# Block 1 to 3 adapter products in float32r from split parts, and the order of Silu and of up's PSUM bank, in a fused LoRA + FP8 gated FFN

## Chip, cores and metric

The kernel runs on one core of one Trainium2 chip. The metric is device time in microseconds of one launch; the figure for the kernel before is the median of 3 runs, 475.9 us (475.79 to 476.99).

## What is computed

For each of 8 sequences of 256 tokens and 1024 features, a LoRA adapter of rank 16 (chosen by an id) replaces the input of a gated feed-forward layer, and the layer's output is added to x:

```
Bx  = x @ B[id].T                     # 1024 -> 16
c   = Bx @ A[id].T                    # 16 -> 1024
xq  = fp8(c / in_scale) * in_scale
hid = silu(xq @ gate.T) * (xq @ up.T) # 1024 -> 2752
out = x + fp8(hid / s) * s @ down.T   # 2752 -> 1024
```

Weights hold values of float8 (e4m3) as float32, and the products Bx and c are float32 in the reference.

## The kernel before, in words

Tokens are laid along the free axis in 4 blocks of 512 (two sequences each, t = 0 to 3), features along the 128 partitions. The 2752 hidden features are NI = 22 chunks of 128, the last with 64.

Each block goes through: B's product (bx), a copy of it to SBUF (bm), A's product (c, in PSUM), and a rounding of c to fp8 with the input scale (xg, 8 feature slabs of 512 tokens). Then for every chunk c and block t, `gate_up` (L580 to L628) does 8 matmuls into a gate bank and 8 into an up bank (y, 128x512), Silu on ACT (g, L610), and the product with up on DVE (hid, L611). The down projection (yd) follows with the same TensorE shapes, and DVE adds x (o, L696).

All TensorE instructions are issued through `multiply` (L469 to L471), which fixes their program order; so all matmuls and weight loads have line L471 in the profile and are told apart by tile names. Other engines' instructions are placed by the framework's scheduler unless they are held with `keep_in_program_order`. Tiles of PSUM come from one pool of 8 banks with one tag: a new tile takes the bank that has been free or is freed first, and its first matmul waits for the reader of the old tile.

B's products use four 32-column strips of the array, A's four 32-row strips, one per sequence (or half of one), so four products stand side by side. In float32, each program instruction of these shows as two matmul and two weight load records.

- Block 0: `two_times_b(0)`, `two_times_a(0, bm)` at the start, with empty products (warm) between.
- Block 1: `two_times_b(1)` is put after 12 of the 16 matmuls of `gate_up(4, 0)`. Each DVE and ACT copy of L517 moves 64 partitions by 128 columns, once straight and once to the other half of the partitions, so that A's products (L531 to L551, 32x128) find all columns. `two_times_a` does 2 parts of four banks each; a part is 16 products of 128 columns. Its banks are rounded by ACT (L529) and DVE (L527) in turn.
- Blocks 2 and 3: `four_times_b` stands after 8 of the 16 matmuls of `gate_up(3, 1)` and `four_times_a` does four banks per pair of feature slabs, 8 products of 16 rows and 256 columns each: pairs 0 and 1 after `gate_up(3, 1)`, pairs 2 and 3 after 8 of 16 matmuls of `gate_up(4, 1)`.

After that come blocks 2 and 3 of chunks 0 to 4, all four blocks of chunks 5 to 21, then down. `NFIRST` is 5.

Loads are issued on SP in the order of the code and wait for one of eight queue slots: x and B and A of block 0, gate and up weights of chunks 0 to 4, B of block 1 (L366), x of block 1 in two pieces of 7 and 1 slabs (L381), A of block 1 (L373), x and B of blocks 2 and 3, A of blocks 2 and 3 (L420). GpSimd only sets constants.

Of the kernel before, what the change touches and what calls it, by code (L numbers as in the profile page):

```python
# [8 lines left out]

F32 = mybir.dt.float32  # L10
BF16 = mybir.dt.bfloat16
FP8 = mybir.dt.float8e4
U16 = mybir.dt.uint16
I32 = mybir.dt.int32
AF = mybir.ActivationFunctionType
ALU = mybir.AluOpType
AX = mybir.AxisListType

P = 128
# [264 lines left out]
def adaln_ffn(  # L284
# [4 lines left out]
    aT: bass.AP,  # L289
    bT: bass.AP,  # L290
    a8: bass.AP,
    b8: bass.AP,
    w_gu: bass.AP,
    w_d: bass.AP,
# [27 lines left out]
    kept = ctx.enter_context(tc.tile_pool(name="kept", bufs=1))  # L322
    wpool = ctx.enter_context(tc.tile_pool(name="w", bufs=5))
    outs = ctx.enter_context(tc.tile_pool(name="outs", bufs=3))
    hid = [kept.tile([P, T], FP8, name=f"hid{c}") for c in range(NI - 1)]


    hid_tail = kept.tile([P, 2, TB], BF16, name="hid_tail")
# [8 lines left out]
    with ExitStack() as fast:  # L337
# [17 lines left out]
        b_four = lora.tile([P, 4 * BROW + R], F32, name="b_four")  # L355
        a_four = lora.tile([P, H], F32, name="a_four")
        nc.gpsimd.memset(a_two[0], 0.0)
        nc.vector.memset(a_two[1], 0.0)
        for b, n in ((b_two[0], 2), (b_two[1], 2), (b_four, 4)):
            nc.vector.memset(b[:, n * BROW :], 0.0)  # L360

# [8 lines left out]
        def load_a_two(t, j, adapter, queue=nc.sync):  # L370
            for g in range(2):
                row = 32 * (2 * g + j) + R * j
                queue.dma_start(  # L373
                    out=a_two[t][row : row + R],
                    in_=a8[bass.ds(adapter * 2 * R + g * R, R), :],
                )

        def load_x(t, k):
            piece, first = x_of(x4, t, k)
            ks = slice(first, first + piece.shape[1])  # L380
            nc.sync.dma_start(out=xs[t][:, ks, :], in_=piece)  # L381
# [25 lines left out]
        adapters = [adapter_of(2 + q, nc.sync) for q in range(6)]  # L407
        for j in range(2):
            load_b(b_two[1], j, adapters[j], nc.sync)
        for k in (0, 7):  # L410
            load_x(1, k)
        for j in range(2):
            load_a_two(1, j, adapters.pop(0))

        for t in (2, 3):
            load_x(t, 0)
            for q in (2 * t - 4, 2 * t - 3):
                load_b(b_four, q, adapters[q], nc.sync)
        for q in range(4):
            nc.sync.dma_start(  # L420
                out=a_four[32 * q : 32 * q + R], in_=aT[bass.ds(adapters[q] * R, R), :]
            )


        sc = b_two[0][:, NH * R : BROW]
# [58 lines left out]
        def times_b(bx, b, n, quads, between=None):  # L484


            for k in range(NH):
                for q, (i, row, t, cols) in enumerate(quads):
                    at = i * BROW + k * R - row
                    multiply(  # L490
                        bx[q][32 * q : 32 * (q + 1)],
                        lhsT=b[:, at : at + 32],
                        rhs=xs[t][:, k, cols],
                        start=(k == 0),
                        stop=(k == NH - 1),
                    )
                if between:
                    between(k)

        def two_times_b(t, between=None):  # L500


            n = SEQ // 2
            quads = [
                (j, R * j, t, slice(at, at + n))
                for half in range(2)
                for j in range(2)
                for at in (j * SEQ + half * n,)
            ]
            bx = [psum.tile([P, n], F32, tag="ps", name=f"bx{half}") for half in range(2)]  # L510
            times_b([bx[q // 2] for q in range(4)], b_two[t], n, quads, between)
            bm = lora.tile([P, 2, n], F32, tag="bm2", name="bm2", bufs=2)
            for other in range(2):
                for half, copy in enumerate((nc.vector.tensor_copy, nc.scalar.copy)):
                    to = half ^ other
                    tc.keep_in_program_order(
                        copy(  # L517
                            bm[64 * to : 64 * (to + 1), other],
                            bx[half][64 * half : 64 * (half + 1)],
                        )  # L520
                    )
            return bm

        def round_to(to, c, engine):
            scale = inv[:, GATE_IN : GATE_IN + 1]
            if engine is nc.vector:
                nc.vector.tensor_scalar(to, c, scale, None, ALU.mult, saturate=False)  # L527
            else:
                nc.scalar.activation(to, c, AF.Copy, scale=scale, saturate=False)  # L529

        def two_times_a(t, bm):  # L531


            n = SEQ // 2
            for part in range(2):
                cs = [psum.tile([P, 2, SEQ], F32, tag="ps", name=f"c{q}") for q in range(4)]
                for other, i in product(range(2), range(2)):
                    for q in range(4):
                        rows = slice(32 * q, 32 * (q + 1))
                        multiply(  # L540
                            cs[q][:, i, bass.ts(q // 2 ^ other, n)],
                            lhsT=a_two[t][rows, bass.ts(2 * part + i, P)],
                            rhs=bm[rows, other],
                            start=True,
                            stop=True,
                        )
                for q in range(4):
                    k = KS * part + 2 * (q // 2)
                    to = xg[t][:, k : k + 2, bass.ts(q % 2, SEQ)]
                    round_to(to, cs[q], nc.vector if q % 2 else nc.scalar)  # L550

        def four_times_b():
            quads = [(q, 0, 2 + q // 2, bass.ts(q % 2, SEQ)) for q in range(4)]
            bx = psum.tile([P, SEQ], F32, tag="ps", name="bx")
            times_b([bx] * 4, b_four, SEQ, quads)
            bm = lora.tile([P, SEQ], F32, tag="bm", name="bm", bufs=2)
            nc.vector.tensor_copy(bm, bx)
            return bm

        def four_times_a(bm, pairs):  # L560
            for i in pairs:
                cs = [psum.tile([P, 2, SEQ], F32, tag="ps", name=f"c{q}") for q in range(4)]
                for k in range(2):
                    for q in range(4):
                        rows = slice(32 * q, 32 * q + R)
                        multiply(
                            cs[q][:, k],
                            lhsT=a_four[rows, bass.ts(2 * i + k, P)],
                            rhs=bm[rows],
                            start=True,  # L570
                            stop=True,
                        )
                for q in range(4):
                    to = xg[2 + q // 2][:, 2 * i : 2 * i + 2, bass.ts(q % 2, SEQ)]
                    round_to(to, cs[q], nc.vector if q % 2 else nc.scalar)
# [5 lines left out]
        def gate_up(c, t, turns=(NH,), between=None):  # L581
# [3 lines left out]
            w = w_of[c]  # L585
            cols = bass.ts(t, TB)
            js = range(1 if tail else 2)
            ys = [psum.tile([P, TB], F32, tag="ps", name=f"y{j}") for j in js]
            steps = []
            for i, n in enumerate(turns):  # L590
                done = sum(turns[:i])
                steps += product(js, range(done, done + n))
            for i, (j, k) in enumerate(steps):
                if between and i == between[0]:
                    between[1]()
                multiply(
                    ys[j],
                    lhsT=high(w[:, k if tail else k // KS * NH + j * KS + k % KS, :]),
                    rhs=xg[t][:, k, :],
                    start=(k == 0),  # L600
                    stop=(k == NH - 1),
                )
            gates, ups = (ys[0], ys[-1]) if not tail else (ys[0][:TAIL], ys[0][TAIL:])
            rows = slice(TAIL, P) if tail else slice(0, P)
            if tail:
                to = lora.tile([P, 2 * TB], FP8, tag="bm", name="tail", bufs=2)[half_of(t), :TB]
            else:
                to = hid[c][:, cols]
            g = work.tile([P, TB], F32, tag="g", name="g")
            nc.scalar.activation(g[rows], gates, AF.Silu, scale=gate_s[: gates.shape[0]])  # L610
            nc.vector.scalar_tensor_tensor(  # L611
                to,
                in0=ups,
                scalar=up_by_down[rows],
                in1=g[rows],
                op0=ALU.mult,
                op1=ALU.mult,
                saturate=False,
            )
            if tail:  # L620
                nc.vector.tensor_copy(hid_tail[half_of(t), t // 2], to)
# [11 lines left out]

        warm = psum.tile([P, TB], F32, tag="ps", name="warm")
        pass_time(warm, 16, TB)
        bm = two_times_b(0, lambda k: pass_time(warm, 4) if k == 6 else None)
        pass_time(warm, 7)
        two_times_a(0, bm)
        gate_up(0, 0, turns=(2, 2, 2, 2))
        for c in range(1, NFIRST - 1):  # L640
            gate_up(c, 0)
        bms = []
        gate_up(NFIRST - 1, 0, between=(12, lambda: bms.append(two_times_b(1))))
        two_times_a(1, bms[0])
        gate_up(0, 1, turns=(2, 2, 2, 2))
        for c in range(1, NFIRST - 2):
            gate_up(c, 1)
# [238 lines left out]
```

## Time and profile before

| | us |
|---|---|
| median of 3 runs | 475.9 |
| profiled execution, first to last instruction | 474.0 |
| bx and c of block 0 end, y begins | 12.1 |
| bx of block 1 begins | 28.9 |
| bx of blocks 2 and 3 begins | 46.0 |
| y of gate and up, 1376 matmuls, mean record | 0.379 |
| ACT rounding of a c bank, 128x512 | 0.69 |
| DVE rounding of a c bank | 0.75 |
| ACT / DVE copy of bx, 64x128 | 0.26 / 0.28 |
| POOL busy in all | 1.0 |

The page gives the span of the profiled execution, 474.0 us at a granted TensorE clock of 1.000, and no other time of that execution; the runs' median is 1.9 us above the span. Records of one engine overlap: a matmul record lasts longer than the distance to the next, so durations of matmuls are not to be added; distances between starts are. A line of the timeline has start, length from first start to last end, engine, line, operation, tiles, count and, in brackets, the idle time before it and what ended it.

### The profile page before, as it was taken

To read this page: it belongs to the slowest core of one execution; us is meant where nothing else is said; L and a number is where in the kernel's file an instruction comes from. 1 tells how busy PE (TensorE), PEld (TensorE's weight loads), DVE (VectorE), ACT (ScalarE), POOL (GpSimd) and SP (SyncE) were. 2 spreads that over 40 slices of the span, in tenths; PEclk is the share of its full clock that TensorE was granted. 3 is DMA by queue.
4 is the path that set the end of the run, shared out by engine and by line. 5 is a ranking of instruction groups with operands and counts; after the bars stand their busy time and mean duration, and the time that the engine had idled before them with its cause. 6 is when DMAs were issued, how large, how long until landed. Compare 5 with 4: busy or idle time off the path is not lost.

```text
span 474.0 us, 6007 instructions
## 1 busy us (share of the span) xinstructions
PE 469.6 (99%) x2514; PEld 217.1 (46%) x2514; DVE 105.6 (22%) x163; ACT 192.5 (41%) x249; POOL 1.0 (0%) x7
## 2 busy tenths in 40 slices
PE   8999999999999999999999999999999999999997
PEld 5454544444444444444444444444444444444444
DVE  2332521212212121222212121232120121031031
ACT  2332438995555745443354544359212022021000
POOL 0000000000000000000000000000000000000000
DMA  8995023322222112222210121133335255163031
GB/s 316 416 406 153 1 90 115 153 89 90 89 89 90 54 45 80 90 89 89 90 57 36 41 62 56 61 100 106 115 135 162 66 184 160 28 212 110 3 116 67
DMA packets 13781, 53.45 MB, mean 113 GB/s; under 512 B 1650, under 2 KB 2930, under 8 KB 10802
## 3 DMA queue, kind: packets, MB, share of 16 engines
q1 hardware_dynamic: 13536, 52.86, 31.8%
q8 instruction: 21, 0.34, 0.3%
q10 hardware_dynamic: 210, 0.14, 0.1%
q14 instruction: 14, 0.11, 0.1%
HBM read 44.60 MB, written 8.39 MB: 112 GB/s over the span
## 4 chain that ended last, share of the span: by engine, by line
PE 96%; DMA 2%; ACTq 0%; ACT 0%; issue 0%; DVE 0%
PE y L471 62%; PE yd L471 32%; DMA w_gu<-w_gu 1%; PE c L471 1%; PE bx L471 1%; DMA a<-a 1%; ACT L307 0%; ACTq L373 0%; ACTq L306 0%; ACTq L366 0%; DVE o L696 0%; ACTq L363 0%; PE count L471 0%
## 5 line engine op out<-in xcount | busy, mean ns | idle before, releaser
L471 PE MATMUL y<-xg,w_gu 128*128 128x512 fp8e4 x1376 | 298.2, 379 | 0.1
L471 PEld LDWEIGHTS <-w_gu 128*128 128x128 bf16 x1376 | 134.1, 98 | 162.8 <-issue 1.3
L471 PE MATMUL yd<-hid,w_d 128*128 128x512 fp8e4 (+2 forms) x693 | 146.0, 373 | 0.0
L610 ACT ACTIVATE g<-y,gate_s 128x512 f32<-128x512 f32 (+1 forms) x88 | 59.8, 681 | 136.3 <-PE y L471 136.3
L611 DVE SCALAR_TENSOR_TENSOR hid<-y,up_by_down,g 128x512 fp8e4<-128x512 f32 x84 | 63.1, 751 | 219.4 <-PE y L471 161.6
L471 PEld LDWEIGHTS <-w_d 128*128 128x128 bf16 x693 | 66.6, 98 | 79.0 <-issue 1.7
L457 ACT ACTIVATE junk<-w_d 128x1408 bf16<-128x1408 uint16 (+1 forms) x16 | 21.2, 1324 | 88.5 <-DMA w_d<-w_d 88.4
L696 DVE SCALAR_TENSOR_TENSOR o<-yd,down_s,x 128x512 f32<-128x512 f32 x28 | 20.0, 748 | 107.3 <-PE yd L471 92.5
L457 ACT ACTIVATE junk<-w_gu 128x2048 bf16<-128x2048 uint16 (+1 forms) x22 | 41.0, 1863 | 0.0
L464 ACT ACTIVATE junk<-hid 128x2048 bf16<-128x2048 fp8e4 x21 | 40.0, 1904 | 0.4
L464 ACT ACTIVATE junk<-xg 128x2048 bf16<-128x2048 fp8e4 x8 | 15.3, 1909 | 0.3
L529 ACT ACTIVATE xg<-c,inv 128x512 fp8e4<-128x512 f32 x16 | 9.7, 688 | 8.6 <-PE c L471 8.6
L527 DVE TENSOR_SCALAR xg<-c,inv 128x512 fp8e4<-128x512 f32 x16 | 10.9, 745 | 2.8 <-PE c L471 2.8
L471 PE MATMUL warm<-zeros 128*128 128x512 bf16 (+1 forms) x27 | 6.6, 404 | 1.2 <-DVE zeros L309 1.2
L696 DVE SCALAR_TENSOR_TENSOR o<-yd,down_s,xg 128x512 f32<-128x512 f32 (+2 forms) x5 | 3.2, 644 | 12.3 <-PE yd L471 12.3
L517 ACT COPY bm<-bx 64x128 f32<-64x128 f32 x4 | 1.0, 262 | 9.2 <-PE bx L471 9.2
L471 PEld LDWEIGHTS <-zeros 128*128 128x128 bf16 x27 | 2.6, 117 | 4.8 <-issue 3.1
L471 PE MATMUL bx<-x,b 128*32 128x128 f32 x128 | 4.3, 276 | 0.1
L471 PE MATMUL c<-bm,a 32*128 32x128 f32 x128 | 4.3, 277 | 0.0
L457 ACT ACTIVATION_READ_ACCUMULATOR junk<-w_gu 128x1 f32 x22 | 4.2, 191 | 0.0
L471 PEld LDWEIGHTS c<-bm,a 32*128 32x128 f32 x128 | 3.9, 186 | 0.5 <-ACT bm L517 0.4
L471 PE MATMUL yd<-hid_tail,w_dt 64*128 64x512 bf16 (+1 forms) x32 | 4.1, 377 | 0.0
(47 smaller groups left out, 41.0 us busy)
## 6 DMA issues: line engine op xcount, KB each, us to landing
w_gu<-w_gu SPq DMA_DIRECT2D x20, 1024.0 KB, 4.8
outT<-o SPq DMA_DIRECT2D x31, 256.0 KB, 2.2
w_d<-w_d SPq DMA_DIRECT2D x8, 704.0 KB, 4.9
w_d<-w_d SPq DMA_DIRECT2D x8, 640.0 KB, 3.9
x<-x SPq DMA_DIRECT2D x2, 2048.0 KB, 11.3
x<-x SPq DMA_DIRECT2D x1, 1792.0 KB, 13.1
w_gu<-w_gu SPq DMA_DIRECT2D x3, 512.0 KB, 4.2
x<-x SPq DMA_DIRECT2D x2, 512.0 KB, 3.9
```

Source lines behind the costliest of these rows:

```text
L457: nc.scalar.activation(junk_like(w), low(w), AF.Copy, accum_out=lows[:rows, column : column + 1])
L464: nc.scalar.activation(junk_like(q), q, AF.Square, accum_out=squares[:rows, column : column + 1])
L471: tc.keep_in_program_order(nc.tensor.matmul(*args, **kwargs))
L517: copy(bm[64 * to : 64 * (to + 1), other], bx[half][64 * half : 64 * (half + 1)],)
L527: nc.vector.tensor_scalar(to, c, scale, None, ALU.mult, saturate=False)
L529: nc.scalar.activation(to, c, AF.Copy, scale=scale, saturate=False)
L610: nc.scalar.activation(g[rows], gates, AF.Silu, scale=gate_s[: gates.shape[0]])
L611: nc.vector.scalar_tensor_tensor(to, in0=ups, scalar=up_by_down[rows], in1=g[rows], op0=ALU.mult, op1=ALU.mult, saturate=False,)
L696: nc.vector.scalar_tensor_tensor(o, in0=y, scalar=down_s, in1=x, op0=ALU.mult, op1=ALU.add)
```

## The change

1. A of block 1 to 3 is loaded with each sequence's 16 rows twice in 32 partitions (arrays `a8_twice`, `a_twice`). GpSimd splits it into float32r parts: lanes 0 to 15 of each 32 get A rounded to float32r, lanes 16 to 31 get the rest. For that it makes a scalar per partition (`lane`, `minus`) with an iota and two DVE instructions.
2. B of block 1 to 3 is copied by GpSimd so that each slab's 16 columns stand twice side by side; B's products then give Bx in both halves of 32 partitions.
3. Bx is split into two float32r parts, bm and rest, by a copy and a subtraction. In block 1 four ACT copies from SBUF then move each part's columns to the other half of the partitions.
4. A's products take float32r operands of 32 rows and 256 columns: per bank two parts times two k (or feature slabs), 16 products for four banks. Blocks 2 and 3 had 8 of 256 columns in float32, block 1 had 16 of 128 columns.
5. Silu is issued in the code right behind the last gate matmul, and the tile of up's bank is taken when its first matmul is issued. For chunks below 5 Silu and hid's product keep their program order.
6. The new tiles lie in the places of hid tiles that are written later. Block 0 is as before.

The diff, cut to its core:

```diff
@@ loads
-        for k in (0, 7):
-            load_x(1, k)
+        load_x(1, 0)
         for j in range(2):
-            load_a_two(1, j, adapters.pop(0))
+            adapter = adapters.pop(0)
+            for g in range(2):
+                load_a_twice(a_two[1], 2 * g + j, a8_twice, adapter * 2 + g)
+        load_x(1, 7)
...
         for q in range(4):
-            nc.sync.dma_start(
-                out=a_four[32 * q : 32 * q + R], in_=aT[bass.ds(adapters[q] * R, R), :]
-            )
+            load_a_twice(a_four, q, a_twice, adapters[q])
@@ GpSimd
+        lane = const.tile([P, 1], I32, name="lane")
+        nc.gpsimd.iota(lane, pattern=[[0, 1]], base=0, channel_multiplier=1)
+        nc.vector.tensor_scalar(lane, lane, R, None, ALU.bitwise_and)
+        minus = const.tile([P, 1], F32, name="minus")
+        nc.vector.tensor_scalar(minus, lane, -1.0 / R, None, ALU.mult)
+        def split(a, parts, cuts=1):
+            n = a.shape[1] // cuts
+            for cols in (bass.ts(i, n) for i in range(cuts)):
+                part = parts[:, cols]
+                nc.gpsimd.tensor_scalar(part, a[:, cols], minus, None, ALU.mult)
+                nc.gpsimd.tensor_tensor(part, a[:, cols], part.bitcast(F32), ALU.add)
+        def twice(b, n, name, slot):
...
+                for copy in range(2):
+                    nc.gpsimd.tensor_copy(to[:, :, copy], row)
...
+        b_twice = [twice(b_two[1], 2, "b_twice", NI - 2)]
+        split(a_two[1], a_parts[0], cuts=2)
+        b_twice.append(twice(b_four, 4, "b_four_twice", NI - 4))
+        for i in range(2):
+            split(a_four[:, bass.ts(i, H // 2)], a_parts[1 + i])
@@ block 1
+        def two_times_b_in_parts():
...
+            for half, copy in enumerate((nc.vector.tensor_copy, nc.scalar.copy)):
+                held(copy(bm[own[half], half], bx[half][own[half]]))
+            for half in range(2):
+                held(
+                    nc.vector.tensor_tensor(
+                        rest[own[half], half],
+                        bx[half][own[half]],
+                        bm[own[half], half].bitcast(F32),
+                        ALU.subtract,
+                    )
+                )
+            for part, half in ((bm, 1), (bm, 0), (rest, 0), (rest, 1)):
+                held(nc.scalar.copy(part[own[1 - half], half], part[own[half], half].bitcast(F32)))
@@ A's products, blocks 1 to 3
+        def times_a_parts(bms, a, at):
+            cs = [psum.tile([P, 2, SEQ], F32, tag="ps", name=f"c{q}") for q in range(4)]
+            for bm, i in product(bms, range(2)):
+                for q in range(4):
+                    rows = slice(32 * q, 32 * (q + 1))
+                    multiply(
+                        cs[q][:, i],
+                        lhsT=a[rows, bass.ts(at + i, P)],
+                        rhs=bm[rows],
+                        start=bm is bms[0] and i == 0,
+                        stop=bm is bms[-1] and i == 1,
+                    )
+            return cs
@@ blocks 2 and 3, behind B's product
             nc.vector.tensor_copy(bm, bx)
-            return bm
...
+            nc.vector.tensor_tensor(rest, bx, bm.bitcast(F32), ALU.subtract)
+            return bm, rest
@@ gate_up
-            ys = [psum.tile([P, TB], F32, tag="ps", name=f"y{j}") for j in js]
+            ys = []
...
+                if j == len(ys):
+                    ys.append(psum.tile([P, TB], F32, tag="ps", name=f"y{j}"))
                 multiply(
...
+                if j == 0 and k == NH - 1:
+                    silu()
```

## The prediction

> **What bounds the kernel now.** I read the busy shares first, then the chain of work that ended last in order of time, then the timeline around the three stretches the change edits.
>
> ```profile
> PE 469.6 (99%) x2514; PEld 217.1 (46%) x2514; DVE 105.6 (22%) x163; ACT 192.5 (41%) x249; POOL 1.0 (0%) x7
> ```
>
> TensorE is busy 469.6 of 474.0 us, so only time taken out of its own queue can shorten the run. The chain (start, us, what) shows how little of that queue the change can touch:
>
> ```profile
> 31.81 2.07 PE c L471 x64
> 33.87 12.19 PE y L471 x56
> 46.07 3.59 PE bx L471 x64
> 49.66 1.83 PE y L471 x8
> 51.49 2.04 PE c L471 x32
> 53.53 1.83 PE y L471 x8
> 55.37 1.94 PE c L471 x32
> 57.30 264.29 PE y L471 x1224
> ```
>
> The A products of block 1 (31.81) and of blocks 2 and 3 (51.49, 55.37) hold 2.07 + 2.04 + 1.94 = 6.05 us, 1.3% of the span. Everything from 57.30 on is gate, up and down matmuls at 264.29 / 1224 = 0.216 us each for 512 columns, 0.42 ns a column; the edit leaves them, so a gain or loss made before 57.30 is carried to the end unchanged. The timeline (start about 0.07 earlier than in the chain) shows who feeds those stretches and who waits:
>
> ```profile
> 30.87 0.60 DVE L517 COPY bm<-bx 64x128 f32<-64x128 f32 x2 [3.65 <-PE bx L471]
> 30.93 0.55 ACT L517 COPY bm<-bx 64x128 f32<-64x128 f32 x2 [2.12 <-PE bx L471]
> 31.74 2.14 PE L471 MATMUL c<-bm,a 32*128 32x128 f32 x64
> 32.93 2.42 ACT L529 ACTIVATE xg<-c,inv 128x512 fp8e4<-128x512 f32 x4 [1.45 <-PE c L471]
> 33.81 12.26 PE L471 MATMUL y<-xg,w_gu 128*128 128x512 fp8e4 x56
> ...
> 51.60 0.75 DVE L611 SCALAR_TENSOR_TENSOR hid<-y,up_by_down,g 128x512 fp8e4<-128x512 f32 x1 [1.45 <-PE y L471]
> 52.59 2.42 ACT L529 ACTIVATE xg<-c,inv 128x512 fp8e4<-128x512 f32 x4 [5.79 <-PE c L471]
> ...
> 55.40 0.69 ACT L610 ACTIVATE g<-y,gate_s 128x512 f32<-128x512 f32 x1 [0.39 <-PE y L471]
> 56.46 2.42 ACT L529 ACTIVATE xg<-c,inv 128x512 fp8e4<-128x512 f32 x4 [0.37 <-PE c L471]
> ```
>
> In all three the TensorE work behind c starts just after the first round of c into xg: 32.93 + 0.69 to 0.79 gives 33.62 to 33.72, and y starts at 33.81; 52.59 + 0.69 = 53.28, y at 53.46; 56.46 + 0.69 = 57.15, y at 57.24. So c is bounded by the rounding engines and PSUM banks as much as by its matmuls.
>
> **What the skill says.** (1) "FP8 and Floating Point Precision", Matmul Precision, TensorE Precision Notes: true FP32 takes four passes; reduced-precision FP32 reads 4 bytes and truncates. The trace agrees on the four: at 51.42 each row group does two 256-column products before the first round, 2 x 4 x 256 x 0.42 ns = 0.86 us, and the round starts 1.17 us after, leaving 0.31 for drain and semaphore; block 1 gives 1.19. No float32r is shown; I take one pass. (2) "TensorE: Matmul & The Clock Gate", Part 3, Packing small matmuls: products in different 32-row groups run together, and a weight load overlaps a matmul of another row group. The trace agrees: the 0.86 us serve four groups at once. (3) "GPSIMD Engine Reference", 2.1 Instruction dispatch: the first call to a freshly loaded kernel pays about 6 us with no instruction shown. The trace has only memsets on POOL (128x512 in 0.53 us). (4) "VectorE: DVE Perf Modes", the errata section: a ScalarE instruction has a fixed part of 172 cycles from PSUM and 224 from SBUF. The trace has only the first: 262 ns for the 64x128 copy.
>
> **A products, blocks 2 and 3.** Per four banks: before, two float32 products per row group, 0.86 us; after, four float32r products (two parts of bm, two k) at 256 x 0.42 = 0.107 us, 0.43 us. The count of products doubles, the passes fall to a quarter. The 128-column float32 products of block 1 already keep a load and 0.107 us of matmul per record going, so I price the loads at nothing; at the 184 ns a 128-column load lasts, four would be 0.74.
> Walk from c at 51.42. The copy bm4 (0.43 measured on the old row) and the new subtraction (estimate 0.45, same shape) run from 49.73 to about 50.7 under eight up matmuls: no cost; without that cover, 0.45. First round: 51.42 + 0.43 + 0.31 = 52.16. The second four banks' last one waits for the hid product of DVE (51.60 to 52.35), so that group runs from 52.41 to 52.84. The gate's bank is freed by the ACT round at 52.16 + 0.69 = 52.85; y starts near 53.00 instead of 53.46: gain 0.46. Eight gate matmuls keep their 1.84: c at 54.84. Its last bank waits for the Silu, 54.94 to 55.63, and ends at 56.1. The first new round is ready at 54.84 + 0.43 + 0.31 = 55.58, ACT is free then, ends 56.27, and up starts at 56.36 instead of 57.24: 0.88 gained in all. Not 2 x 0.86: DVE, the Silu and the rounds are late next. Bounds: 0.15 to 1.1.
> **A products, block 1.** Two copies per engine become, in a fixed order, a PSUM copy each on DVE and ACT, two DVE subtractions and four ACT copies from SBUF. They are covered by four up matmuls (30.77 to 31.63) only. ACT: 30.93 + 0.28 for the first, then four at 0.32 (0.28 spacing measured, plus 52 cycles, estimate 0.04, from the page in 4) and some 0.1 for a wait on its own result: last copy ends near 32.6. DVE is ready by 31.8. The rest half of c starts at 32.68, two products per group 0.22, plus 0.31: round at 33.2 against 32.93. The sixteen products of the second half lie under that round. y at 34.07: loss 0.25. Bounds: with copies at 0.26 and no wait, gain 0.3; with 0.4 a copy, loss 0.6. Queued behind these copies on ACT and DVE are only block 1's own rounds and hid.
> **Loads and POOL.** SP issues A for block 1 doubled, 4 x 64 KB for 4 x 32 KB, and ahead of the last x piece, which so goes from 15.57 to about 23.2 (a load there waited for a queue slot until 23.17).
>
> ```profile
> x<-x SPq DMA_DIRECT2D x1, 1792.0 KB, 13.1
> x<-x SPq DMA_DIRECT2D x1, 256.0 KB, 13.3
> b<-b SPq DMA_DIRECT2D x2, 68.0 KB, 9.1
> ```
>
> x lands at 15.10 + 13.1 = 28.2; behind it 0.25 MB of A and 0.25 MB of x at the 0.41 MB a us of that stretch land by 28.9 and 29.5. The last x is read at 28.88 + 7 x 0.213 = 30.4, so it is hidden, by 0.9. B is there at 23.8; POOL's four copies (estimate 0.3 each from the memset) end by 25.1, needed at 28.88. Its split of A starts at 28.9: two scalings at 0.35 and one addition at 0.65 (estimate, 2.6 cycles an element, the GPSIMD page, 3.1) end at 30.3, needed at 31.63. Blocks 2 and 3: B lands near 41.5, A, now 0.5 MB, near 43; POOL ends by 47.5, needed at 51.4. Cost nothing; if POOL is twice as slow, 0.1.
> **Silu, up's bank, hid tiles.** Silu already stands behind the gate on ACT in these stretches; up's bank taken late only changes which eviction a product waits for, counted above. Later blocks have eight banks for four matmul groups: nothing. The DVE memset removed had nothing waiting.
> **Start.** POOL now loads a library and does an iota at about 1.6; two DVE instructions wait for it, and behind them on DVE stand the bm copies of block 0 (9.59), then c, xg and every y. At 6 us plus issue it ends near 8: hidden, by 1.5.
>
> **Sum.** -0.88 + 0.25 = -0.63 us against the profiled span of 474.0, so 473.4. The median of the runs is 475.9; the 1.9 us between is outside the span or between executions, and I leave it: 475.3.
>
> **Rivals.** (a) Slower: the library load. Against it: the price and 1.5 us of slack. For it: the price is from elsewhere, and DMA is 80 to 90% busy then. From 9.6 it delays block 0; 0.24 us of that is absorbed where c=1 waits for its weights (y from 15.58 to 15.82). An iota at 12 gives 475.3 + 2.4 - 0.24 = 477.5. (b) Slower: float32r runs at four passes: 1.72 per four banks, two more times 0.86 in each of three stretches, less the waits it covers, about 5: 480.7. (c) No change: weight loads bind, 0.74 per four banks: first stretch gains 0.2, second 0.1, block 1 loses 0.4: 476.0. For it: same row group, and a load lasts 184 ns. (d) Faster: short ACT copies and no bank wait: 0.3 + 1.1 = 1.4, 474.4.
>
> **Numbers.** About 0.3%, 1.4 us, is what a measurement can tell from no change. Forecast 475.3: 0.50. (c) 0.11. (d) 0.14. (a) 0.18, with late splits on POOL in it. (b) 0.07. So faster 0.14, same 0.61, slower 0.25. The range 474.2 to 477.7 leaves out (b) and the far ends of (a) and (d).
>
> **What would show it.** c records one per product, 0.43 us per four banks; y at 53.0 and up at 56.4; block 1's y at 34.1 with an idle TensorE before the rest products; the iota's end before 9.5. Wrong: two records per product, a DVE wait on POOL at 9 us, or TensorE waiting for POOL at 28.9, 31.7 or 51.4.

## The result and the profile after

The changed kernel takes 475.39 us (median of 18 runs, 475.13 to 475.61); the kernel before, run beside it, 476.02 (18 runs, 475.69 to 477.04). The ratio is 0.9985, with a 95% interval of 0.9978 to 0.9992: a gain of 0.15%. That is half of what the prediction named as the least that one can tell from no change, but with 18 runs of each kernel the interval leaves no change out. The profiled execution took 475.24 us and spans 473.4, so 1.84 lies outside the span; the span went down by 0.6 and the medians by 0.63.

The busy shares of the kernel after, to be read against the same row of before:

```profile
PE 468.0 (99%) x2482; PEld 215.5 (46%) x2482; DVE 106.0 (22%) x166; ACT 193.4 (41%) x252; POOL 12.9 (3%) x28
```

TensorE has 32 records fewer: 96 c products in float32r now leave one record each (96), where 64 float32 products left two each (128). POOL has gone from 1.0 to 12.9 us.

The chain of work that ended last, kernel after (start, us, what):

```profile
29.88 1.83 POOL a_parts L456 x2
31.70 0.70 POOL a_parts L457
...
32.45 0.82 PE c L526 x16
33.27 0.75 DVE xg L615
...
34.07 12.26 PE y L526 x56
...
51.86 0.76 DVE hid L732
...
52.67 0.73 PE c L526 x12
53.40 1.83 PE y L526 x8
55.23 1.51 PE c L526 x29
56.75 264.29 PE y L526 x1224
```

Before, this part of the chain was TensorE alone. Now it goes through POOL and DVE's rounding (block 1), and through DVE's hid product, whose PSUM bank the first stretch of blocks 2 and 3 waits for. The last line has the same 264.29 us and 1224 matmuls as before, but begins at 56.75 instead of 57.30: the whole gain is made before it and carried to the end.

A stretch is the time from the first product of c to the first y matmul behind it. The timeline of the kernel after around the three stretches (start, length, engine, line; in brackets the idle time before and what ended it):

```profile
30.99 0.26 ACT L598 CAST bm_parts<-bx 64x128 fp32r<-64x128 f32 x1 [2.12 <-PE bx L526]
31.67 1.42 POOL L457 TENSOR_TENSOR a_parts<-a,a_parts 128x256 fp32r<-128x256 f32 x2
31.81 0.61 ACT L609 CAST rest<-rest 64x128 fp32r<-64x128 f32 x2
32.45 0.51 PE L526 MATMUL c<-bm_parts,a_parts 32*128 32x256 f32 x8 [0.59 <-POOL a_parts L457]
32.79 0.40 PE L526 MATMUL c<-rest,a_parts 32*128 32x256 f32 x8
33.23 2.42 ACT L617 ACTIVATE xg<-c,inv 128x512 fp8e4<-128x512 f32 x4 [0.81 <-PE c L526]
...
51.68 0.51 PE L526 MATMUL c<-bm,a_parts 32*128 32x256 f32 x8
52.46 2.42 ACT L617 ACTIVATE xg<-c,inv 128x512 fp8e4<-128x512 f32 x4 [5.41 <-PE c L526]
52.66 0.29 PEld L526 LDWEIGHTS c<-bm,a_parts 32*128 32x128 f32 x5 [0.33 <-DVE hid L732]
53.33 1.90 PE L526 MATMUL y<-xg,w_gu 128*128 128x512 fp8e4 x8
...
55.16 0.51 PE L526 MATMUL c<-bm,a_parts 32*128 32x256 f32 x8
55.94 2.42 ACT L617 ACTIVATE xg<-c,inv 128x512 fp8e4<-128x512 f32 x4
56.01 0.29 PEld L526 LDWEIGHTS c<-bm,a_parts 32*128 32x128 f32 x5 [0.19 <-ACT g L703]
56.68 3.63 PE L526 MATMUL y<-xg,w_gu 128*128 128x512 fp8e4 x16
```

The two PEld lines (weight loads, which stand ahead of their products) show the second group of four banks held up: in the first stretch by DVE's hid product, in the second by Silu on ACT (g).

The balance, from starts in the timelines of the two kernels:

| part | before | after | difference |
|---|---|---|---|
| bx of block 1 begins | 28.88 | 28.94 | +0.06 |
| bx of block 1 to y behind its c | 4.93 | 5.13 | +0.20 |
| first stretch of blocks 2 and 3, c to y | 2.04 | 1.65 | -0.39 |
| second stretch, c to y | 1.94 | 1.52 | -0.42 |
| y of the 264.29 us begins | 57.24 | 56.68 | -0.56 |

The first row is scatter: over all the kernels below, bx began between 28.77 and 28.96. The other rows are in both traces on work that the change edits. So blocks 2 and 3 gain 0.81 and block 1 gives 0.20 of it back. The experiments ask whether these parts are independent, what held block 1, what bounds the two other stretches, and whether the edit of `gate_up` has any part in it. Each ratio below is to the kernel before, run on the same chip.

### The profile page after: what moved, and what is told of

Same layout as the page of the kernel before. It is cut to its first block, busy times and chain, and to the rows that moved or that the text cites. A ratio compares the mean times of both kernels' runs of the same rounds, so it can differ in the third digit from the quotient of the medians.

```text
span 473.4 us, 5970 instructions
## 1 busy us (share of the span) xinstructions
PE 468.0 (99%) x2482; PEld 215.5 (46%) x2482; DVE 106.0 (22%) x166; ACT 193.4 (41%) x252; POOL 12.9 (3%) x28
## 3 DMA queue, kind: packets, MB, share of 16 engines
q1 hardware_dynamic: 13664, 53.25, 32.4%
## 4 chain that ended last, share of the span: by engine, by line
PE 92%; DMA 5%; POOL 1%; DVE 0%; ACTq 0%; ACT 0%; issue 0%; SPq 0%; POOLq 0%; DVEq 0%
PE y L526 59%; PE yd L526 32%; DMA w_gu<-w_gu 2%; DMA a<-a_twice 2%; DMA a<-a 1%; PE bx L526 1%; PE c L526 1%; POOL a_parts L456 0%; ACT L310 0%; DVE hid L732 0%; SPq L408 0%; DVE xg L615 0%; POOL a_parts L457 0%; ACTq L385 0%; ACTq L309 0%
## 5 line engine op out<-in xcount | busy, mean ns | idle before, releaser
L732 DVE SCALAR_TENSOR_TENSOR tail<-y,up_by_down,g 64x512 fp8e4<-64x512 f32 x4 | 3.0, 756 | 4.9 <-ACT g L703 4.8
L519 ACT ACTIVATION_READ_ACCUMULATOR junk<-hid 128x1 f32 x21 | 3.9, 187 | 0.0
L526 PE MATMUL bx<-x,b_four_twice 128*32 128x256 f32 x64 | 3.7, 380 | 0.0
```

The costliest lines, as they stand in the source:

```text
L519: nc.scalar.activation(junk_like(q), q, AF.Square, accum_out=squares[:rows, column : column + 1])
L526: tc.keep_in_program_order(nc.tensor.matmul(*args, **kwargs))
L732: nc.vector.scalar_tensor_tensor(to, in0=ups, scalar=up_by_down[rows], in1=g[rows], op0=ALU.mult, op1=ALU.mult, saturate=False,)
```

## Experiments

### The parts by themselves

Three kernels. `b23only` takes block 1 back to float32, with its loads as before:

```diff
...
-        gate_up(NFIRST - 1, 0, between=(12, lambda: bms.append(two_times_b_in_parts())))
-        two_times_a_parts(bms[0])
+        gate_up(NFIRST - 1, 0, between=(12, lambda: bms.append(two_times_b(1))))
+        two_times_a(1, bms[0])
```

> Block 1 as in the kernel before (float32, its A loads and copies); blocks 2 and 3 and gate_up as in the changed kernel. Theory (blocks 2 and 3 gain 0.8 us, block 1 gives back 0.2): y of block 1 starts 2.07 after c as before, c to y of blocks 2 and 3 stays at 1.65 and 1.52 us, the span is some 0.2 below the changed kernel's 473.4, about 473.2. Rival (block 1 brings part of the gain, or costs nothing): span 473.4 or more.

`b1only` takes blocks 2 and 3 back to float32, with 16 rows and A loaded once:

```diff
...
-            rest = in_place_of_hid(NI - 13, [P, SEQ], F32R, "rest4")
-            nc.vector.tensor_tensor(rest, bx, bm.bitcast(F32), ALU.subtract)
-            return bm, rest
+            return bm
...
-                cs = times_a_parts(bms, a_parts[1 + i // 2], 2 * (i % 2))
+                cs = [psum.tile([P, 2, SEQ], F32, tag="ps", name=f"c{q}") for q in range(4)]
+                for k in range(2):
+                    for q in range(4):
+                        rows = slice(32 * q, 32 * q + R)
+                        multiply(
+                            cs[q][:, k],
+                            lhsT=a_four[rows, bass.ts(2 * i + k, P)],
+                            rhs=bms[rows],
+                            start=True,
+                            stop=True,
+                        )
```

> Blocks 2 and 3 as in the kernel before (float32, 16 rows); block 1 and gate_up as in the changed kernel. Theory: y of block 1 at 34.07 as in the changed kernel, c to y of blocks 2 and 3 back at 2.04 and 1.94; the span is 474.2, 0.2 above the kernel before. Rival (block 1 gains too, the loss seen there is scatter of the loads): span at or under 474.0.

`gateup` is the kernel before with only the new `gate_up`:

```diff
-            ys = [psum.tile([P, TB], F32, tag="ps", name=f"y{j}") for j in js]
+            ys = []
...
+                if j == len(ys):
+                    ys.append(psum.tile([P, TB], F32, tag="ps", name=f"y{j}"))
...
+                if j == 0 and k == NH - 1:
+                    silu()
```

> The kernel before with the new gate_up alone: Silu right behind the gate, up's bank taken late, both held in order for chunks under 5; all products in float32. Theory (this part does nothing: Silu stood there already and the same evictions free the same banks): span 474.0 within 0.1, c to y of 2.04 and 1.94. Rival (the second gain of 0.42 us is up's bank, not float32r): the second stretch falls to about 1.5, span 473.6.

| kernel | median | ratio to before | span | bx to y, block 1 | two stretches |
|---|---|---|---|---|---|
| b23only | 475.03 | 0.9983 [0.9976, 0.9989] | 473.1 | 4.93 | 1.65, 1.52 |
| b1only | 476.16 | 1.0011 [1.0002, 1.0019] | 474.2 | 5.13 | 2.04, 1.94 |
| gateup | 475.80 | 1.0000 [0.9992, 1.0008] | 474.0 | 4.92 | 2.04, 1.94 |

Each stretch has the length of the version that it holds, to 0.01 us, whatever the others do. The change of the spans, -0.9 and +0.2, adds up to -0.7 for the -0.6 of both. Blocks 2 and 3 are the gain, block 1 is a loss whose interval just excludes no change, and the order of Silu and of up's bank does nothing with float32 products. The old order with float32r products was not run. What speaks against an effect there: in the second stretch of the kernel before, eight c products of different banks stand behind each other with no wait for a rounding (the eighth bank's products begin by 56.28, the first rounding of that stretch ends at 57.15), so of the 8 banks up held none in the old order either.

### Who holds block 1: GpSimd's split of A

In the trace after, two things end together: GpSimd's split at 32.40 (bm products at 32.45) and ACT's last rest copy at 32.42 (rest products by 32.79). `dvesplit` takes the first away by letting DVE split A of block 1, at a time when DVE is idle:

```diff
-        def split(a, parts, cuts=1):
+        def split(a, parts, cuts=1, engine=nc.gpsimd):
...
-                nc.gpsimd.tensor_scalar(part, a[:, cols], minus, None, ALU.mult)
-                nc.gpsimd.tensor_tensor(part, a[:, cols], part.bitcast(F32), ALU.add)
+                engine.tensor_scalar(part, a[:, cols], minus, None, ALU.mult)
+                engine.tensor_tensor(part, a[:, cols], part.bitcast(F32), ALU.add)
...
-        split(a_two[1], a_parts[0], cuts=2)
+        split(a_two[1], a_parts[0], cuts=2, engine=nc.vector)
```

> The changed kernel with A of block 1 split by DVE (two scalings and two additions of 128x256, some 1.3 us from 29.7) where GpSimd took 3.3 us from 29.88; blocks 2 and 3 stay on GpSimd. Theory (the rest products of block 1 wait for the four ACT copies as the prediction had it, and GpSimd's late split only keeps the bm products from running before them): bm products at 31.7, rest products at 32.48 instead of 32.68, y of block 1 at 33.85 instead of 34.07. Rival (GpSimd is the whole cause): rest products follow at once, y at 33.5 or earlier. Rival (neither: rounding engines): y stays at 34.07.

Measured: 475.07 us, 0.9985 [0.9977, 0.9993], span 473.1; bx to y 4.92. The timeline of `dvesplit`, same columns:

```profile
29.81 0.62 DVE L456 TENSOR_SCALAR a_parts<-a,minus 128x256 fp32r<-128x256 f32 x2 [2.60 <-DMA a<-a_twice]
30.34 0.75 DVE L457 TENSOR_TENSOR a_parts<-a,a_parts 128x256 fp32r<-128x256 f32 x2
31.72 0.66 PE L526 MATMUL c<-bm_parts,a_parts 32*128 32x256 f32 x8
32.40 0.30 PEld L526 LDWEIGHTS c<-rest,a_parts 32*128 32x128 f32 x8 [0.23 <-ACT rest L609]
```

DVE makes the four instructions of the split in 1.28 us (29.81 to 31.09). GpSimd takes 3.21 (29.88 to 33.09), and 2.52 up to the end of its first addition (32.40), which the first bm products need. With DVE's split they start 0.73 earlier, as soon as ACT has copied bm. But the rest products start only where the copies of rest end, at 32.40, and y starts at 33.78; from bx to y that is 4.92, as before the change. Both starts are within 0.08 of the theory's 32.48 and 33.85, and both rivals fell. So GpSimd's split is the 0.20 that block 1 loses, and the chain of ACT copies is why there is no gain behind it.

The profiled executions carry this reading: from bx to y it takes 5.13 to 5.16 us in the four kernels with GpSimd's split and these products (the changed kernel, `b1only`, `spread`, `at12`). The medians can't tell `dvesplit` from the changed kernel; the ratio is 0.9985 for both. One thing was not run: the code issues the first half's addition ahead of the second half's scaling, and the trace has both scalings first. In the order of the code the first half would be ready at 29.88 + 0.93 + 0.73 = 31.54 (an estimate from GpSimd's own times), before the bm products are due.

`dvesplit_shared` also gives the last of the four copies to DVE:

```diff
-            for part, half in ((bm, 1), (bm, 0), (rest, 0), (rest, 1)):
-                held(nc.scalar.copy(part[own[1 - half], half], part[own[half], half].bitcast(F32)))
+            for part, half, copy in (
+                (bm, 1, nc.scalar.copy),
+                (bm, 0, nc.scalar.copy),
+                (rest, 0, nc.scalar.copy),
+                (rest, 1, nc.vector.tensor_copy),
+            ):
+                held(copy(part[own[1 - half], half], part[own[half], half].bitcast(F32)))
```

> As dvesplit, and the last of the four copies of block 1 (rest, second half) goes to DVE. Theory: the rest is ready at 32.15 instead of 32.42, y of block 1 at 33.6, so block 1 takes no more than in the kernel before (33.81); DVE's hid product and its first round start 0.2 later and may hold y to 33.7. Rival (ACT copies aren't the bound once GpSimd is out): the same y as dvesplit.

Measured: 474.96 us, 0.9982 [0.9975, 0.9990], span 473.0; bx to y 4.74, 0.19 less than before the change; y begins at 33.64, where 33.6 to 33.7 was expected. The timeline of `dvesplit_shared`:

```profile
31.91 0.22 DVE L614 CAST rest<-rest 64x128 fp32r<-64x128 f32 x1
...
32.97 0.29 PEld L526 LDWEIGHTS c<-bm_parts,a_parts 32*128 32x128 f32 x5 [0.37 <-DVE hid L737]
```

The rest copies end at 32.13 and their products begin at 32.18. The next wait is the one of the other stretches: the second four banks lack one bank, which DVE's hid product, queued behind the copy, still reads.

### What bounds blocks 2 and 3

In the changed kernel eight c banks in a row find only some banks free, and the others wait for hid, Silu or a rounding. `spread` puts the four groups of four banks apart in the gate and up matmuls of one block, instead of two and two:

```diff
...
-        four_times_a(bms[1], (0, 1))
-        gate_up(NFIRST - 1, 1, between=(8, lambda: four_times_a(bms[1], (2, 3))))
+        four_times_a(bms[1], (0,))
+        gate_up(
+            NFIRST - 1,
+            1,
+            between={
+                5: lambda: four_times_a(bms[1], (1,)),
+                10: lambda: four_times_a(bms[1], (2,)),
+            },
+        )
+        four_times_a(bms[1], (3,))
```

> The changed kernel with the four groups of A products of blocks 2 and 3 put apart: before gate_up(4,1), after 5 and after 10 of its 16 matmuls, and behind it, so that each has 1.1 us of gate and up matmuls between. Theory (the two stretches of 1.65 and 1.52 us hold 4 x 0.43 of products and the rest is waiting for banks, hid, Silu and roundings): four stretches of about 0.63 each, 2.5 in all for 3.17, span 0.65 lower, 472.8. Rival (the rest is the cost of products and of changing the array's tiling, or weight loads): 3.17 or more, with two more changes of tiling perhaps 3.5, span 473.4 to 473.8.

Measured: 475.23 us, 0.9990 [0.9984, 0.9997], span 473.2. The chain of `spread`:

```profile
51.77 0.68 PE c L526 x16
52.46 1.19 PE y L526 x5
53.64 0.67 PE c L526 x13
...
55.50 0.67 PE c L526 x14
...
57.58 0.67 PE c L526 x14
```

No other engine stands in it any more: the four groups take 0.69 + 0.67 + 0.68 + 0.67 = 2.71 us in the timeline, for 1.65 + 1.52 = 3.17. `spread` was expected to be worth 0.65; the profile shows 0.25. Five y matmuls between two groups take 1.18 where 5 x 0.216 = 1.08, so each of the two more changes between c and y costs 0.10 on that side, which takes 0.2 off the 0.46. The runs can't tell `spread` from the changed kernel: their intervals overlap widely.

The waits themselves were more than 0.46, because the two more changes also cost time inside the groups. In the records the products of the four row groups start together, within 20 ns where no wait sets them apart, and the next four follow 0.118 us later. A group of 16 is so 4 x 0.118 = 0.47, and by itself it lasts 0.68: a change to c and back costs 0.21. Two groups in a row without a wait would take 8 x 0.118 + 0.21 = 1.15. The stretches of the changed kernel took 1.65 and 1.52, so 0.50 and 0.37 of them are waits.

The kernel before had next to none. The view of its waits lists none for a TensorE matmul from 25 to 60 us; its float32 records come 0.216 us after each other, again four at a time, and 8 x 0.216 + 0.21 = 1.94 is the whole of its second stretch, while the first has 0.10 more. So float32r took 0.79 out of each stretch, 1.58 in all, and 0.77 of that went into waits that were not there before.

`at12` goes the other way, and moves the second stretch behind 12 of 16 matmuls, four later:

```diff
-        gate_up(NFIRST - 1, 1, between=(8, lambda: four_times_a(bms[1], (2, 3))))
+        gate_up(NFIRST - 1, 1, between=(12, lambda: four_times_a(bms[1], (2, 3))))
```

> The changed kernel with pairs 2 and 3 of blocks 2 and 3 put after 12 instead of 8 of the 16 matmuls of gate_up(4,1). Theory (PSUM banks bind: up now holds a bank, so the last of the eight c banks waits for the first round, which ends 1.5 us after c starts): the stretch takes 1.5 + 0.43 + 0.2 = 2.1 us instead of 1.52, span 474.0. Rival (the stretch waits for Silu and for up's own bank only, both past by then): 1.25 us, span 473.1.

One run, 475.95 us, span 474.1; the stretch lasts 2.17 for 1.52. The line of its timeline that says why:

```profile
57.59 0.29 PEld L526 LDWEIGHTS c<-bm,a_parts 32*128 32x128 f32 x5 [0.86 <-ACT xg L617]
```

By then up has its bank too, so the second group waits for the first rounding of ACT. The bank theory held; the rival, that the stretch waits only for Silu and up's bank and so falls to 1.25 at a later place, fell.

### Is it one pass

The prediction took one pass for float32r; four, or products bound by their weight loads, were rivals. `cols128` does each product of 256 columns as two of 128, the same columns with twice the loads:

```diff
-                    multiply(
-                        cs[q][:, i],
-                        lhsT=a[rows, bass.ts(at + i, P)],
-                        rhs=bm[rows],
-                        start=bm is bms[0] and i == 0,
-                        stop=bm is bms[-1] and i == 1,
-                    )
+                    for n in range(2):
+                        multiply(
+                            cs[q][:, i, bass.ts(n, P)],
+                            lhsT=a[rows, bass.ts(at + i, P)],
+                            rhs=bm[rows, bass.ts(n, P)],
+                            start=bm is bms[0] and i == 0 and n == 0,
+                            stop=bm is bms[-1] and i == 1 and n == 1,
+                        )
```

> The changed kernel with each float32r product of 256 columns made as two of 128. Theory (one pass whatever the columns; the price is then a weight load for each): 8 products per row group and four banks, between 0.43 and 8 x 0.107 = 0.86 us for 0.43, span 473.4 to 475.5. Rival (under 256 columns float32r runs at the four passes of float32): 8 x 0.213 = 1.7 us for four banks, some 1.3 us more in each of six groups less what waits cover, span 478 to 481.

Measured: 477.10 us, 1.0029 [1.0017, 1.0041], span 474.5. Its chain:

```profile
52.02 2.02 PE c L526 x64
...
55.88 1.95 PE c L526 x64
```

The stretches are back at the lengths of float32 (2.02 and 1.95 for 2.04 and 1.94), with twice the records in place of two per product. Four products of 128 columns, one per row group, follow the four before them after 0.112 us, and with 256 columns after 0.118. Half the columns save next to nothing, so a product costs a row group some 0.115 us at either width. At 256 columns that is about the 0.107 of one pass (256 x 0.42 ns); two passes would be 0.21 and four 0.43, so more than one is ruled out. What sets the floor at 128 columns stays open: a weight load for each product and a second pass (2 x 128 x 0.42 = 0.107) would both fit. The float32 records of block 1 in the kernel before, also 128 columns wide, come 0.112 apart as well.

### All of it together

`joined` has DVE's split, the shared copies and the spread groups, with the diffs shown above.

> The changed kernel with all three edits that helped: A of block 1 split by DVE, the last copy of rest on DVE, and the four groups of blocks 2 and 3 spread. Theory (the gains lie in different stretches and add: 0.4 in block 1, 0.25 in blocks 2 and 3): from bx of block 1 to y 4.74 us, four groups of 0.68, span 472.8, median 0.65 under the changed kernel. Rival (what one stretch gives is lost in the next wait): span 473.0 or more.

Measured: 474.76 us (14 runs), 0.9978 [0.9970, 0.9986], span 472.9. In the profiled executions it beats the kernel before by 1.1 and the changed kernel by 0.5 in the span. Its median is 1.02 below the kernel before on its chip, where the changed kernel's was 0.63 below: 0.39 apart where 0.65 was expected, and the intervals of the two ratios overlap. The four groups took 0.67 to 0.68 each. Block 1 fell short: bx to y 4.88, not 4.74. In this execution A landed later and DVE's split ended at about 31.25, after bx, so DVE's first copy of bx began at 31.17 for 30.95, and the hid product and its bank came later in turn (c's wait for it ended at 33.18 for 32.97). That fits a split on DVE without slack, where the landing of A decides; one execution shows it.

## Why the prediction was right, point by point

- **Size and place.** The span of 473.4 and the change of -0.63 came out as written, from parts of nearly the right size: -0.81 for -0.88 in blocks 2 and 3, and +0.20 (+0.26 with the later bx) for +0.25 in block 1. The time outside the span (1.84 for 1.9) was rightly left alone.
- **The opening reading.** "So c is bounded by the rounding engines and PSUM banks as much as by its matmuls" does not hold for the kernel before. There y began just after the first rounding by coincidence: the products alone fill the second stretch, and all but 0.10 of the first. It holds for the changed kernel. The forecast didn't suffer, because its walk was made with the new products.
- **Products in one pass.** 0.47 us for four banks, taken as 0.43; a first rounding 0.78 after c, taken as 0.74. One record per product, as named there. The four-pass rival fell: the stretches would have grown. Rival (c), bound by loads, fell as priced, with 0.74 for four banks; but the floor that `cols128` shows at 128 columns (0.112) lies close under what 256 columns take (0.118).
- **First stretch.** A gain of 0.39 where 0.46 was forecast. The first rounding and the wait for hid came as in the walk. The last hand-off did not: the walk lets y wait for ACT's first rounding. That ended at 52.46 + 0.69 = 53.15, and y began 0.18 later, where a TensorE wait that ends on ACT is over in 0.05 (`at12`: 57.54 and 57.59). So y followed the second group of products. From its restart at 52.66 to y that took 0.67, as long as a group by itself, where the walk has 0.43 + 0.16.
- **Second stretch.** A gain of 0.42, as forecast; c to up took 1.52, as in the walk. Here y came 0.67 behind the restart at 56.01 and 0.05 behind the end of ACT's first rounding (56.63), so the trace can't say which of the two let it go. "Not 2 x 0.86" was right: the two stretches of the changed kernel hold some 0.87 of waits.
- **Block 1.** y at 34.07, as forecast, but for another reason. The step that failed is GpSimd's: "two scalings at 0.35 and one addition at 0.65 ... end at 30.3 ... Cost nothing; if POOL is twice as slow, 0.1". A landed at 29.67, not 28.9, and GpSimd began at 29.88; the two scalings took 1.83, not 0.70, and run ahead of the first addition, as the prediction had them; the addition took 0.73. So the first half was ready at 32.4, 2.1 late, and the bm products, due from 31.6, waited for it. The addition's price was near; the scaling's, which no row of the trace before showed and which was taken as cheaper than the addition, was 2.6 times too low. Neither the landing (1.0 late at GpSimd's start) nor the scalings (1.1 more) would have cost anything alone, against some 1.4 of slack. TensorE waiting for POOL at 31.7 is among the prediction's own signs of being wrong, and the trace has it, 0.59 before 32.45.
- **Block 1, the copies on ACT.** The estimate for ACT was good: copies at 0.30 and the last one done at 32.42, for 0.32 and 32.6; the surplus of a copy from SBUF over one from PSUM, worked out as 0.04 from the Trainium skill ("VectorE: DVE Perf Modes", the errata section), measures 0.036. By itself the ACT chain brings y to 33.78, level with before (`dvesplit`), so it takes what float32r gives and doesn't add the 0.25. That these two errors, a loss of 0.25 on ACT that did not come and one of 0.20 on GpSimd that was priced at nothing, met in one number is luck.
- **Silu, up's bank.** Nothing, shown by `gateup` for float32 products. Rival (d) needed short ACT copies and no bank wait; both waits are in the trace.
- **Start.** Rival (a), the library load, didn't show as a delay. The timeline of the kernel after:

```profile
1.57 0.13 POOL L443 IOTA lane<- 128x1 int32 x1
...
6.75 0.15 DVE L444 TENSOR_SCALAR lane<-lane 128x1 int32<-128x1 int32 x1
```

The iota runs at 1.57 for 0.13 us, and DVE comes to `lane` at 6.75 in its own order. The Trainium skill ("GPSIMD Engine Reference", 2.1 Instruction dispatch) states about 6 us for the first call after a load; no run here shows it.

- **Loads.** SP's doubled loads did not delay bx beyond its scatter; but A, queued behind x's first piece, landed 0.8 later than worked out (29.67 for 28.9). That counts only because the split of A hangs on it. The splits of A for blocks 2 and 3 ended at 50.1 (the last two additions run from 47.60 for 2.51 us), not by 47.5, and still 1.5 ahead of their first use at 51.68.

## What to carry to other kernels

Where a stretch is a relay of engines, faster matmuls give back only what no wait takes: here 0.39 us were removed from four banks, twice in each stretch, and half of that was gained, though the kernel before had hardly a wait there. So ask which waits the faster matmuls will uncover, not only which are there; walking the hand-offs one by one gave each stretch to within 0.07. Work put on an idle engine is free only if the landing of its input plus that engine's own time for each instruction ends before the result is needed. So price it on that engine, instruction by instruction, and give a low and a high price when no row shows it. When two waits end together, take one away in a run before calling either the cause: the number alone was right here for the wrong engine.

## What the runs showed of the hardware

- GpSimd's multiplication by a per-partition scalar is slower than its addition of two tiles: 927 against 730 ns for 128x256, 1564 against 1276 for 128x512 (kernel after). The difference of the two sizes is 2.5 and 2.1 ns a column, with 0.29 and 0.18 us besides. DVE took 350 and 418 ns for the 128x256 ones (`dvesplit`).
- Products of 32 rows in float32r leave one record, where a float32 product leaves two. Four of them, one per row group, start within 20 ns where no wait sets them apart, and the next four follow after 0.118 us with 256 columns (kernel after) and 0.112 with 128 (`cols128`).
- A group of 16 such products with 256 columns, alone between full matmuls, lasts 0.68 us, 0.21 more than the products, and the y matmuls beside it lose another 0.10 (`spread`).
- ACT's 64x128 copy takes 297 ns from SBUF and 261 from PSUM (kernel after).
